# A decoder block on one core: the order of loads, diagonal operands and stores in its opening

## The chip, the core and the metric

The kernel runs on one core of a Trainium2 chip. The core has five engines that run their own queues of instructions side by side: TensorE (PE, with its weight loads as PEld) multiplies matrices, VectorE (DVE) and ScalarE (ACT) work element by element and read the PSUM banks that PE writes, GpSimd (POOL) works element by element on SBUF alone, and SyncE (SP) issues the transfers (DMAs). The metric is the device time of one execution in microseconds (us); smaller is better. All data is float32.

## What is computed

The reference takes x of shape (4, 2048, 512) and a context of shape (4, 77, 512) and applies one decoder layer of three parts, each on a layer norm and each added to x:

```python
x = x + recurrence(layernorm(x))      # step t: z = V (A*z + Vinv_dt x_t), output 2*Re(z); T=4 steps
x = x + cross_attention(layernorm(x)) # 16 heads of 32, 77 keys, softmax, Wq Wk Wv Wo (512x512)
h = layernorm(x) @ W_exp + b_exp      # 512 -> 2048
h = gelu(butterfly(h, up_weights) + up_bias)
x = x + butterfly(h, down_weights) @ W_con + b_con + down_bias
```

A butterfly is eleven stages of 2x2 mixtures over 2048 features. No non-linear step lies between W_exp and the first butterfly, nor between the second and W_con, so each pair is one 512x2048 or 2048x512 matrix, but this matrix has to be computed from its factors before it can be used.

## The kernel before

The 2048 rows of each of the four steps are worked on in 16 turns of 128 rows. `front` (L504) does the recurrence and the attention of a turn and makes the normalised input of the feed-forward part; `feed_forward` (L634) does the two large products. In turn u, `feed_forward(u)` is on PE while `front(u+1)` is advanced in small steps between its products (`step`, L643). All large products use Strassen's form with seven products in place of eight on half-sized blocks; the sums and differences of weight blocks that it needs are made once and kept in DRAM: `up7` (L769, one tensor for each of eight block columns, seven blocks each), `dn7` (seven tensors) and `wq7`.

Before the first turn can run there is an **opening** (L775 to L835). It makes the recurrence's taps (`_recurrence_taps`, L68), keys and values (`_keys_values`, L136), the two combined matrices (`_prepare`, L224) and the front of turn 0. All four are Python generators; each `next` on one of them emits its instructions up to its next `yield`. The lists of `run(...)` calls and the loop at L819 thus write the order out by hand. In this part PE, SP and POOL run in exactly that order (L775); DVE and ACT are ordered by the compiler's scheduler. After the opening PE is ordered by hand only for the first four block columns of turn 0 (L706).

`_prepare` goes through these steps:

- L285 to L293: W_exp is multiplied by the low seven butterfly stages; L299 to L305: transposes.
- L308 to L319: four groups g. For each, four PSUM banks are filled with products against `bd`, 16 diagonal matrices made at L298 by `diagonals` (L248), and evicted into `wup`, which then holds the first combined matrix. The turn counter in `evict` (L241) gives 2 of 5 evictions to DVE, 3 of 5 to ACT. SP loads a quarter of W_con after each group (L318).
- L321: `diagonals` once more, all 16 at once, into `bdd` for the second matrix. Their place is a tile of the tag `xt1` (L782).
- L330 to L344: the seven blocks of the first matrix. The first block of each column goes straight from `wup` to DRAM (L331, 8 transfers of 128 KB). For each of eight columns p, POOL (L335, L336) and DVE (L337, L338) make four sums in a ring of three places in `spare`, and SP stores them (L339, 512 KB). Two more blocks go straight out in 16 transfers (L343). `spare` is the room of the output weights `wo`, which are loaded later (L823).
- L346 to L353: 16 steps (n = 0 to 15 in the loop at L819) with `bdd`; L363 to L384: 16 steps (n = 16 to 31) of transposes L360 and products L369, with one group of four stores of sums every fourth step (`t1`, `t3`, `t2`, `n4` at L378 to L381, stores at L383). L385 closes it.

Beside it runs turn 0's front: its query product (`seven`, L488, evicted at L536 and L539), the scores (L557 to L567, row maxima and subtraction on DVE, exponent on ACT, scaling on POOL), the transposed probabilities `pt` (L575, tag `pt`, one buffer, shared with the query weights `wq`), the output product (evicted at L607) and a last norm (`norm_stats` L415, rows L446, transposes L455).

Then the preparation's pool is closed and others are opened in its room (L836 to L840): the activations, three weight buffers, and `ffn` with the tile `tb` of right-hand sums (`combine`, L622, L628 to L631). `up_head` (L665) takes a weight buffer and loads one block column of `up7` into it (L667), then emits the products 1, 6 and 5 of that column; the right side of product 1 is the normalised input itself, those of 6 and 5 are in `tb`. `up_mid` emits 2 and 7. The x of turn 1 is loaded at n = 18 (L829) into the place that `bdd` had.

```python
for n, _ in enumerate(prep):
    if n not in (3, 6, 9, 12, 23, 24, 25, 26):
        next(first, None)
    ...
    if n == 18:
        xts[1] = load_x(1)
```

Of the kernel before, what the change touches and what calls it, by code (L numbers as in the profile page):

```python
# [17 lines left out]
P = 128  # L18
# [49 lines left out]
def _recurrence_taps(nc, pool, psum, ssm_vec, ssm_vt, ssm_vinv, gt):  # L68


    vec = pool.tile([NS, 3], F32, name="vec")
    vt = pool.tile([NS, 3, NS], F32, name="vt")
    pz = pool.tile([NS, 2, 2 * NS], F32, tag="pz", bufs=2, name="pz")
    nc.sync.dma_start(out=vec, in_=ssm_vec)
    nc.sync.dma_start(out=vt[:, 0:2, :], in_=ssm_vt)
    nc.sync.dma_start(out=pz, in_=ssm_vinv)
    yield

    e = pool.tile([NS, 2], F32, name="e")
    _exp(nc, pool, e, vec[:, 0:2], 2)  # L80
    dt = e[:, 0:1]
    th = pool.tile([NS, 2], F32, name="th")
    nc.vector.tensor_tensor(th[:, 0:1], e[:, 1:2], dt, ALU.mult)
    nc.vector.tensor_scalar(th[:, 0:1], th[:, 0:1], -1.0, None, ALU.mult)
    nc.vector.tensor_tensor(th[:, 1:2], vec[:, 2:3], dt, ALU.mult)
    mag = pool.tile([NS, 1], F32, name="mag")
    _exp(nc, pool, mag, th[:, 0:1], 1)

    k = pool.tile([NS, 1], F32, name="k")
    r = pool.tile([NS, 2], F32, name="r")  # L90
    nc.vector.tensor_scalar(k, th[:, 1:2], 0.5 / math.pi, MAGIC, ALU.mult, ALU.add)
    nc.vector.tensor_scalar(k, k, -MAGIC, None, ALU.add)
    prev = th[:, 1:2]
    for c in _split(2.0 * math.pi, 8, 5):
        nc.vector.scalar_tensor_tensor(r[:, 0:1], k, -c, prev, ALU.mult, ALU.add)
        prev = r[:, 0:1]
    nc.vector.tensor_scalar(r[:, 0:1], r[:, 0:1], -3.1415925, 3.1415925, ALU.max, ALU.min)
    nc.vector.tensor_scalar(r[:, 1:2], r[:, 0:1], 0.5, None, ALU.mult)
    sn = pool.tile([NS, 2], F32, name="sn")
    nc.scalar.activation(sn, r, AF.Sin)  # L100
    az = pool.tile([NS, 2], F32, name="az")
    nc.vector.tensor_tensor(az[:, 0:1], sn[:, 1:2], sn[:, 1:2], ALU.mult)
    nc.vector.tensor_scalar(az[:, 0:1], az[:, 0:1], -2.0, 1.0, ALU.mult, ALU.add)
    nc.vector.tensor_tensor(az[:, 0:1], az[:, 0:1], mag, ALU.mult)
    nc.vector.tensor_tensor(az[:, 1:2], sn[:, 0:1], mag, ALU.mult)

    nc.vector.tensor_scalar(vt[:, 2, :], vt[:, 1, :], -1.0, None, ALU.mult)
    nc.vector.tensor_scalar(pz, pz, dt, None, ALU.mult)
    nc.gpsimd.memset(gt, 0.0)
    for j in range(T):  # L110
        ps = psum.tile([P, 512], F32, tag="c", name="ps_g")
        nc.tensor.matmul(ps[:, 0:NS], lhsT=pz[:, 0, :], rhs=vt[:, 0, :], start=True, stop=False)
        nc.tensor.matmul(ps[:, 0:NS], lhsT=pz[:, 1, :], rhs=vt[:, 2, :], start=False, stop=True)
        for h in range(2):
            if j + h < T:
                q = slice(h * NS, (h + 1) * NS)
                nc.vector.tensor_scalar(gt[q, j + h, :], ps[q, 0:NS], 2.0, None, ALU.mult)
        if j == T - 1:
            break
        rr = psum.tile([P, 512], F32, tag="f", name="ps_rr")[0:NS, 0 : 2 * NS]  # L120
        ri = psum.tile([P, 512], F32, tag="f", name="ps_ri")[0:NS, 0 : 2 * NS]
        nc.tensor.matmul(rr, lhsT=vt[:, 0, :], rhs=pz[:, 0, :], start=True, stop=False)
        nc.tensor.matmul(rr, lhsT=vt[:, 2, :], rhs=pz[:, 1, :], start=False, stop=True)
        nc.tensor.matmul(ri, lhsT=vt[:, 0, :], rhs=pz[:, 1, :], start=True, stop=False)
        nc.tensor.matmul(ri, lhsT=vt[:, 1, :], rhs=pz[:, 0, :], start=False, stop=True)
        nxt = pool.tile([NS, 2, 2 * NS], F32, tag="pz", bufs=2, name="pz_next")
        ti = pool.tile([NS, 2, 2 * NS], F32, tag="ti", name="ti")
        nc.vector.tensor_scalar(ti[:, 0, :], ri, az[:, 1:2], None, ALU.mult)
        nc.vector.scalar_tensor_tensor(nxt[:, 0, :], rr, az[:, 0:1], ti[:, 0, :], ALU.mult, ALU.subtract)
        nc.vector.tensor_scalar(ti[:, 1, :], rr, az[:, 1:2], None, ALU.mult)  # L130
        nc.vector.scalar_tensor_tensor(nxt[:, 1, :], ri, az[:, 0:1], ti[:, 1, :], ALU.mult, ALU.add)
        pz = nxt
        yield
# [90 lines left out]
def _prepare(nc, keep, pool, room, late, banks, dram, ident, wexp_t, up_low, up_high, up_bias, dn_low, dn_high, wcon,  # L224
# [11 lines left out]
    t = wdn  # L236
    mask = pool.tile([P, sub], F32, name="mask")
    nc.vector.tensor_reduce(mask, ident.rearrange("p (b i) -> p i b", i=sub), AX.X, ALU.add)
    turn = [0]

    def evict(out, ps):  # L241
        turn[0] += 1
        if turn[0] % 5 in (0, 2):
            nc.vector.tensor_copy(out, ps)
        else:
            nc.scalar.copy(out, ps)

    def diagonals(hp, place):  # L248
        for m in range(NB):
            keep(nc.vector.tensor_tensor(place[:, m, :].rearrange("p (b i) -> p b i", b=NB),  # L250
                                         hp[:, m, :].unsqueeze(2).to_broadcast([P, NB, sub]),
                                         mask.unsqueeze(1).to_broadcast([P, NB, sub]), ALU.mult))
        return [place[:, m, :] for m in range(NB)]
# [51 lines left out]
            yield  # L305
    el = _low_products(nc, keep, low, True, False)
    pb = banks()
    for g in range(4):  # L308
        for c in range(NC):
            ps = banks()  # L310
            for j in range(4):
                nc.tensor.matmul(ps.rearrange("p (k m) -> p m k", m=4)[:, j], lhsT=t[:, 4 * g + j, c * P : (c + 1) * P],
                                 rhs=bd[4 * g + j], start=j == 0, stop=True, skip_group_check=True)
            evict(wup[:, c, :].rearrange("p (k m) -> p k m", m=NB)[:, :, 4 * g : 4 * g + 4], ps.rearrange("p (k m) -> p k m", m=4))
        for j in range(4):
            m = 4 * g + j
            nc.tensor.matmul(pb[:, m : m + 1], lhsT=bd[m], rhs=b2[:, m : m + 1], start=True, stop=True)
        nc.sync.dma_start(out=t[:, 4 * g : 4 * g + 4, :], in_=wcon.rearrange("(p m) d -> p m d", m=NB)[:, 4 * g : 4 * g + 4, :])  # L318
        yield  # L319
    nc.vector.tensor_copy(b2, pb[:, 0:NB])  # L320
    bdd = diagonals(hp_dn, late())  # L321
    h, k = HID // 2, NC // 2

    def quarters(p):
        q = slice(p * P, (p + 1) * P)
        a11, a12 = wup[:, 0:k, q], wup[:, k:NC, q]
        q = slice(h + p * P, h + (p + 1) * P)
        return a11, a12, wup[:, 0:k, q], wup[:, k:NC, q]

    for p in range(NB // 2):  # L330
        nc.sync.dma_start(out=up7[p][:, 0], in_=quarters(p)[0])  # L331
    for p in range(NB // 2):
        a11, a12, a21, a22 = quarters(p)
        s = spare[:, p % 3 * 1024 : p % 3 * 1024 + 1024].rearrange("p (i k q) -> p i k q", i=4, k=k)
# [3 lines left out]
        nc.vector.tensor_tensor(s[:, 3], a12, s[:, 1], ALU.subtract)  # L338
        nc.sync.dma_start(out=up7[p][:, 3:7], in_=s)  # L339
        if p == NB // 2 - 1:  # L340
            for n in range(NB // 2):
                for i in (1, 2):
                    nc.sync.dma_start(out=up7[n][:, i], in_=quarters(n)[2 * i - 1])  # L343
        yield  # L344
    nc.sync.dma_start(out=brow[1, :].rearrange("(p m) -> p m", m=NB), in_=b2)
    for c in range(NC):  # L346
# [10 lines left out]
    def turned(b):  # L357
# [2 lines left out]
            nc.tensor.transpose(ps[:, c * P : (c + 1) * P], wup[:, c, b * P : (b + 1) * P], ident)  # L360
        evict(t[:, b, :], ps)

    for n in range(2):  # L363
        turned(order[n])
    for n, b in enumerate(order):
# [7 lines left out]
        if n % 4 == 3:  # L373
# [4 lines left out]
            nc.vector.tensor_tensor(t1, b12, b11, ALU.subtract)  # L378
            nc.gpsimd.tensor_tensor(t3, b22, b12, ALU.subtract)
            nc.vector.tensor_tensor(t2, b22, t1, ALU.subtract)  # L380
            nc.vector.tensor_tensor(n4, b21, t2, ALU.subtract)  # L381
            for i, w in ((0, b11), (1, b21), (2, b22), (4, t1), (6, t3), (5, t2), (3, n4)):
                nc.sync.dma_start(out=dn7[i][:, f, :], in_=w)  # L383
        yield  # L384
# [5 lines left out]
def kernel(ctx: ExitStack, tc: tile.TileContext, x, ctx_t, ssm_vec, ssm_vt, ssm_vinv, wq_t, wk_t, wv_t,  # L390
# [243 lines left out]
    def feed_forward(u, xt, rhs, other):  # L634
# [28 lines left out]
            nc.scalar.activation(out, x, AF.Gelu, bias=hbias[:, b : b + 1])  # L663

        def up_head(p):  # L665
            w = weights([P, 7, 2, P], "w_up")
            nc.sync.dma_start(out=w, in_=up7[p])  # L667
            a, b, c = (bank(g).rearrange("p (x t q) -> p x t q", x=2, q=P)[:, 0] for g in "abc")
            live[p] = (w, a, b, c)
            up(p, 1, a, True)  # L670
# [95 lines left out]
        turn[0] = (turn[0] + 1) % 3  # L766
        return psum.tile([P, 512], F32, tag="abc"[turn[0]], name="ps_p")

    up7 = [dram.tile([P, 7, 2, P], F32, name=f"up7_{p}") for p in range(NB // 2)]  # L769
    wq7 = dram.tile([P, 7, NC // 2, D // 2], F32, name="wq7")  # L770
    dn7 = [dram.tile([P, NB // 2, D // 2], F32, name=f"dn7_{i}") for i in range(7)]
    xts = {}
    ready = []
    E = mybir.EngineType
    with ExitStack() as stack, tc.manual_schedule(engines={E.PE, E.SP, E.Pool}):  # L775
        pool = stack.enter_context(tc.tile_pool(name="prep", bufs=1))
# [12 lines left out]
        def run(*gens):  # L789
            for g in gens:  # L790
                next(g, None)
# [5 lines left out]

        with tc.tile_pool(name="taps", bufs=1) as tp:
            taps = _recurrence_taps(nc, tp, psum, ssm_vec, ssm_vt, ssm_vinv, gt)
            run(taps, keys, prep, keys)  # L800
            xts[0] = load_x(0)
            next(prep)
            quarter_loads(wq, wq_t, (0, 1, 3, 6))
# [13 lines left out]
            run(prep, first)  # L817
        run(first, first)
        for n, _ in enumerate(prep):  # L819
            if n not in (3, 6, 9, 12, 23, 24, 25, 26):  # L820
                next(first, None)
            if n == 3:
                quarter_loads(wo, wo_t, (0, 1, 2, 6))  # L823
# [1 line left out]
                nc.gpsimd.tensor_tensor(wo[:, 6], wo[:, 2], wo[:, 6], ALU.subtract)  # L825
                nc.gpsimd.tensor_tensor(wo[:, 5], wo[:, 2], wo[:, 4], ALU.subtract)
                nc.gpsimd.tensor_tensor(wo[:, 3], wo[:, 1], wo[:, 5], ALU.subtract)
            if n == 18:
                xts[1] = load_x(1)  # L829
        for _ in first:  # L830
            pass
        db = work.tile([P, D], F32, tag="xn", name="db")
# [89 lines left out]
```

## Time and profile before

| | us |
|---|---|
| median of 3 runs (2638.39 to 2641.36) | 2640.1 |
| the profiled execution | 2640.16 |
| its span in the trace | 2638.4 |
| PE busy | 2566.2 (97%) |
| DVE busy | 1449.0 (55%) |
| POOL busy | 950.1 (36%) |
| ACT busy | 809.9 (31%) |
| DMA: 333.6 MB, share of the 16 engines on SP's queue | 36.0% |

The times inside the opening, from the timelines:

| event | us from the start |
|---|---|
| first product of keys (L150) starts | 9.07 |
| the matmuls L312 of the first matrix start | 83.30 |
| the diagonals for the second matrix (L250), DVE | 101.35 |
| the scores of turn 0 (L557) start | 119.2 |
| the products L350 of the second matrix start | 130.6 |
| the load of the x of turn 1 is issued | 172.07 |
| last product of the output projection ends | 190.0 |
| last preparation product on PE ends | 212.1 |
| first feed-forward product starts | 224.55 |

How to read it: busy time of PE is modelled and includes pipelining, so what is worth looking for is not its share but the places where PE stands still, and what ended each wait. A line of a timeline gives start and length in us, engine, source line, operation, output<-inputs, shape and count; in brackets stands how long the engine had been idle before it, and the instruction whose end released it. Where an instruction waits for several events, only the one that came last by the profile is named, and it can be the wrong one. The granted clock of PE is given in tenths of full speed.

### The profile page before, as it was taken

Reading aid. Unit: us, or ns where it says so; the run is one execution under the profiler, and the core shown is the slowest. Engines: PE = TensorE matmul, PEld = TensorE weight load, DVE = VectorE, ACT = ScalarE, POOL = GpSimd, SP = SyncE. Lnnn points to the kernel's source line nnn. Section 1 sums busy time; section 2 is a strip of 40 time slices with the busy share of each in tenths; the row PEclk is TensorE's granted clock in tenths of the full one; section 3 lists DMA queues with packets and bytes.
Section 4 is the critical chain, followed back from the end, with each engine's and each line's share of the span. In section 5 each row is a group of like instructions: output and inputs, shape, how many; then the busy total and the mean of one; then the engine's idle time right before and its main releaser. Section 6 shows DMA issues by size and latency. Waiting matters only on the chain.

```text
span 2638.4 us, 37437 instructions
## 1 busy us (share of the span) xinstructions
PE 2566.2 (97%) x14536; PEld 2182.0 (83%) x14536; DVE 1449.0 (55%) x3355; ACT 809.9 (31%) x1470; POOL 950.1 (36%) x1025
## 2 busy tenths in 40 slices
PE   7887999999999999999999999999999999999999
PEld 5775888888888888888888888888888888888888
DVE  6666645545564554556455455645545564554531
ACT  2332414124241412424141342414234241423420
POOL 4332342515234251523425152342515234251523
PEclk9898999999999999999999999999999999999999
DMA  5536243242424324242432424233242423323243
GB/s 177 199 109 211 93 136 132 87 150 96 160 92 136 132 87 150 96 160 92 136 132 87 150 97 160 92 134 132 88 150 97 160 92 133 131 91 134 96 133 139
DMA packets 95394, 333.60 MB, mean 126 GB/s; under 512 B 15601, under 2 KB 49521, under 8 KB 78065
## 3 DMA queue, kind: packets, MB, share of 16 engines
q1 hardware_dynamic: 95218, 331.21, 36.0%
q8 instruction: 116, 1.90, 0.3%
q14 instruction: 60, 0.49, 0.1%
HBM read 297.61 MB, written 33.57 MB: 126 GB/s over the span
## 4 chain that ended last, share of the span: by engine, by line
PE 83%; DVE 6%; ACT 5%; issue 1%; DMA 0%; ACTq 0%; DVEq 0%; SPq 0%
PE ps_a L726 13%; PE ps_b L658 10%; PE ps_b L726 8%; PE ps_w L499 7%; PE ps_a L658 7%; PE ps_c L658 7%; PE ps_q L499 7%; PE ps_c L726 6%; PE ps_sc L557 5%; PE ps_pt L579 4%; PE ps_s L514 3%; PE ps_o L589 2%; PE ps_t L455 2%; ACT L563 1%; ACT L663 1%; DVE st L420 1%
## 5 line engine op out<-in xcount | busy, mean ns | idle before, releaser
L658 PE MATMUL ps_b<-tb,w_up 128*128 128x256 f32 x1536 | 397.7, 380 | 0.0
L726 PE MATMUL ps_a<-w_dn,a 128*128 128x256 f32 x1536 | 373.0, 380 | 0.0
L701 POOL TENSOR_TENSOR s<-a,a 128x256 f32<-128x256 f32 x128 | 93.0, 727 | 675.9 <-ACT a L663 453.5
L658 PEld LDWEIGHTS ps_b<-tb,w_up 128*128 128x128 f32 x1536 | 287.7, 190 | 39.4
L663 ACT ACTIVATE a<-a,hbias 128x256 f32<-128x256 f32 x384 | 193.6, 508 | 406.5 <-DVE a L696 277.2
L726 PEld LDWEIGHTS ps_a<-w_dn,a 128*128 128x128 f32 x1536 | 282.4, 190 | 41.6 <-issue 3.0
L658 PE MATMUL ps_a<-xnt,w_up 128*128 128x256 f32 x1024 | 264.2, 381 | 12.0 <-DMA w_up<-up 12.0
L726 PE MATMUL ps_c<-w_dn,s 128*128 128x256 f32 x1024 | 248.6, 379 | 0.0
L456 ACT COPY xnt<-ps_t 128x512 f32<-128x512 f32 x128 | 73.7, 587 | 523.1 <-PE ps_t L455 523.1
L567 POOL TENSOR_TENSOR pr<-pr,sm 128x1232 f32<-128x1232 f32 x64 | 144.0, 2250 | 248.8 <-DVE sm L566 243.9
L658 PEld LDWEIGHTS ps_a<-xnt,w_up 128*128 128x128 f32 x1024 | 192.0, 191 | 37.9 <-issue 12.2
L726 PEld LDWEIGHTS ps_c<-w_dn,s 128*128 128x128 f32 x1024 | 188.7, 190 | 27.8
L607 DVE TENSOR_TENSOR xt<-ps_w,xt 128x512 f32<-128x512 f32 x96 | 66.1, 689 | 213.6 <-PE ps_w L499 147.0
L557 PE MATMUL ps_sc<-kbd,qt 128*128 128x308 f32 x512 | 174.4, 439 | 5.9 <-DVE pr L562 5.7
L714 POOL TENSOR_TENSOR xt<-xt,ybias 128x256 f32<-128x256 f32 x128 | 99.4, 810 | 223.1 <-DVE xn L446 223.0
L563 ACT ACTIVATE pr<-pr 128x308 f32<-128x308 f32 x256 | 111.1, 457 | 136.2 <-DVE pr L562 135.7
L579 PE MATMUL ps_pt<-ident,pr 128*77 128x128 f32 x1024 | 143.8, 276 | 8.6 <-ACT a L663 4.7
L499 PE MATMUL ps_q<-xnt,wq 128*128 128x256 f32 x640 | 151.4, 380 | 0.0
L579 PEld LDWEIGHTS ps_pt<-ident,pr 128*77 128x77 f32 x1024 | 117.6, 147 | 40.5 <-ACT a L663 11.0
L499 PEld LDWEIGHTS ps_q<-xnt,wq 128*128 128x128 f32 x640 | 122.1, 191 | 16.7
L672 ACT COPY p<-ps_a 128x256 f32<-128x256 f32 x128 | 47.7, 373 | 277.7 <-PE ps_a L658 277.7
L658 PE MATMUL ps_c<-tb,w_up 128*128 128x256 f32 x512 | 132.5, 381 | 0.0
(199 smaller groups left out, 4586.5 us busy)
## 6 DMA issues: line engine op xcount, KB each, us to landing
w_up<-up SPq DMA_DIRECT2D x128, 896.0 KB, 4.6
w_dn<-dn SPq DMA_DIRECT2D x112, 1024.0 KB, 4.8
wq<-wq SPq DMA_DIRECT2D x16, 1792.0 KB, 8.5
xt<-in_x SPq DMA_DIRECT2D x16, 1024.0 KB, 5.3
out<-xt SPq DMA_DIRECT2D x64, 256.0 KB, 4.7
wdn<-in_wexp_t SPq DMA_DIRECT2D x4, 1024.0 KB, 10.3
wdn<-in_wcon SPq DMA_DIRECT2D x4, 1024.0 KB, 5.1
up<-wo SPq DMA_DIRECT2D x8, 512.0 KB, 2.6
```

The costliest lines, as they stand in the source:

```text
L456: nc.scalar.copy(xnt[:, :, t, :], ps)
L499: nc.tensor.matmul(tiles[key][:, r, :], lhsT=lhs(i, r, k), rhs=rhs(i, r, k), start=key == i and r == 0 and k == 0, stop=k == 1, skip_group ...
L514: nc.tensor.matmul(ps[:, 2 * i : T, f * NS : (f + 1) * NS], lhsT=xpt[:, i, c * (P // NS) + f, :], rhs=gt[:, 0 : T - 2 * i, :], start=i == ...
L557: nc.tensor.matmul(ps[:, 0 : 4 * NK], lhsT=qt[:, g, t, :], rhs=kbd[:, t, g, :], start=True, stop=True)
L563: nc.scalar.activation(pg, pg, AF.Exp, scale=1.0 / math.sqrt(DH))
L567: nc.gpsimd.tensor_tensor(pr, pr, sm.unsqueeze(2).to_broadcast([P, NH, NK]), ALU.mult)
L579: nc.tensor.transpose(pt_ps[0:NK, j, :], pr[:, 4 * g + j, :], ident)
L658: nc.tensor.matmul(ps, lhsT=w[:, c, :], rhs=rhs[i - 1][:, c], start=first and c == 0, stop=c == 1, skip_group_check=True)
L663: nc.scalar.activation(out, x, AF.Gelu, bias=hbias[:, b : b + 1])
L701: nc.gpsimd.tensor_tensor(s1, a21, a22, ALU.add)
L714: nc.gpsimd.tensor_tensor(r, r, ybias[:, d], ALU.add)
L726: nc.tensor.matmul(ps[:, t, :], lhsT=act[p][lhs[i]][:, t, :], rhs=w[:, p, :], start=first and p == 0 and t == 0, stop=p == h - 1, skip_gro ...
```

## The change

It touches the opening, and one place in `up_head`.

- The generator of the taps yields once more after the load of `vec`, and the first `run` calls it twice: the loads of the context and of Wk are issued between `vec` and the other two.
- `diagonals` can make some of the 16. Those for the second matrix are made in four lots of four, each at the head of one of the four groups of the loop at L308.
- `up7` becomes one DRAM tensor. A function `plain` stores one of the three unchanged blocks for all eight columns in two transfers (one for each half of the contraction): 6 transfers in place of 24.
- From the last 16 steps on, DVE gets 2 of 6 evictions in place of 2 of 5. The last of the four differences, `n4`, goes from DVE to POOL.
- In the loop over n the steps at which the front is not advanced change: 4, 8, 12 and 22 to 26 in place of 3, 6, 9, 12 and 23 to 26.
- At n = 17 the weights of the first block column are loaded into a tile of the tag `pt`; `up_head` takes them in place of a weight buffer and a load, once. The x of turn 1 is loaded after the loop.

```diff
     nc.sync.dma_start(out=vec, in_=ssm_vec)
+    yield
     nc.sync.dma_start(out=vt[:, 0:2, :], in_=ssm_vt)
...
-    turn = [0]
+    turn, share = [0], [5]
...
-        if turn[0] % 5 in (0, 2):
+        if turn[0] % share[0] in (0, 2):
...
-    def diagonals(hp, place):
-        for m in range(NB):
+    def diagonals(hp, place, some=slice(0, NB)):
+        for m in range(NB)[some]:
...
+    place = late()
     for g in range(4):
+        bdd = diagonals(hp_dn, place, slice(4 * g, 4 * g + 4))
         for c in range(NC):
...
-    bdd = diagonals(hp_dn, late())
...
-    for p in range(NB // 2):
-        nc.sync.dma_start(out=up7[p][:, 0], in_=quarters(p)[0])
+    def plain(i, c, x):
+        for n in range(k):
+            nc.sync.dma_start(out=up7[:, :, i, n, :].rearrange("b p q -> p b q"),
+                              in_=wup[:, c + n, x : x + h].rearrange("p (b q) -> p b q", q=P))
+
+    plain(0, 0, 0)
...
-            for n in range(NB // 2):
-                for i in (1, 2):
-                    nc.sync.dma_start(out=up7[n][:, i], in_=quarters(n)[2 * i - 1])
+            plain(1, k, 0)
+            plain(2, k, h)
...
+    share[0] = 6
     for n in range(2):
         turned(order[n])
...
-            nc.vector.tensor_tensor(n4, b21, t2, ALU.subtract)
+            nc.gpsimd.tensor_tensor(n4, b21, t2, ALU.subtract)
...
-            w = weights([P, 7, 2, P], "w_up")
-            nc.sync.dma_start(out=w, in_=up7[p])
+            if early:
+                w = early.pop()
+            else:
+                w = weights([P, 7, 2, P], "w_up")
+                nc.sync.dma_start(out=w, in_=up7[p])
...
-    up7 = [dram.tile([P, 7, 2, P], F32, name=f"up7_{p}") for p in range(NB // 2)]
+    up7 = dram.tile([NB // 2, P, 7, 2, P], F32, name="up7")
...
-            run(taps, keys, prep, keys)
+            run(taps, keys, taps, prep, keys)
...
-            if n not in (3, 6, 9, 12, 23, 24, 25, 26):
+            if n not in (4, 8, 12, 22, 23, 24, 25, 26):
...
-            if n == 18:
-                xts[1] = load_x(1)
+            if n == 17:
+                early.append(work.tile([P, 7, 2, P], F32, tag="pt", bufs=1, name="w_first"))
+                nc.sync.dma_start(out=early[0], in_=up7[0])
+        xts[1] = load_x(1)
```

More of the change, by code (lines that the diff above doesn't have):

```diff
@@ L773 @@
     ready = []
+    early = []
     E = mybir.EngineType
```

## The prediction

> **What bounds the kernel now.** I read the 40 slices first, then the table of stretches, then the timelines of PE (TensorE), DVE (VectorE), POOL (GpSimd) and SP (the DMA queue) over the first 260 us, and last the chain of waits around the stalls found there. From the page, the slices of PE and its granted clock:
>
> ```profile
> PE   7887999999999999999999999999999999999999
> PEclk9898999999999999999999999999999999999999
> ```
>
> Only the first four slices (66 us each) are below 9. The table (columns: stretch; length, busy us and counts of PE, weight loads, DVE, ACT, POOL; clock, DMA share, GB/s) says where:
>
> ```profile
> 100.00:120.00 20.00, 14.76 (x62) 12.07 (x61) 13.87 (x32) 2.46 (x3) 9.88 (x13) 0.83 0.56 187
> 120.00:140.00 20.00, 13.80 (x82) 8.63 (x82) 16.57 (x36) 5.25 (x11) 7.60 (x6) 0.83 0.52 184
> 200.00:220.00 20.00, 8.09 (x33) 4.64 (x31) 14.46 (x42) 4.59 (x8) 3.78 (x3) 0.84 0.77 228
> 260.00:400.00 140.00, 139.64 (x801) 119.18 (x801) 75.14 (x167) 44.24 (x79) 52.60 (x53) 1.00 0.31 108
> ```
>
> From 260 us on PE is full, and the change edits none of that work. What can move is the opening: 26 us of PE idle in three 20-us stretches. The timelines name three stalls of PE. **Stall 1**, at 104.8:
>
> ```profile
> 109.88 3.75 PE L499 MATMUL ps_q<-tq,wq 128*128 128x256 f32 x8 [5.09 <-DVE qt L536]
> ...
> 101.35 7.44 DVE L250 TENSOR_TENSOR bd<-hp_dn,mask 128x128 f32<-128x128 f32 x16
> ```
>
> PE waits for the eviction L536, which stands on DVE behind all 16 diagonal products. **Stall 2**, at 201.4, waits for normalised rows L446 at the end of a DVE queue without a gap; **stall 3**, at 212.6, for the first FFN weights:
>
> ```profile
> 205.92 0.66 PE L455 MATMUL ps_t<-ident,xn 128*128 128x128 f32 x4 [4.50 <-DVE xn L446]
> 224.55 2.04 PE L658 MATMUL ps_a<-xnt,w_up 128*128 128x256 f32 x4 [11.97 <-DMA w_up<-up]
> ```
>
> The chain of waits shows what precedes stall 3's end, and DVE's timeline what else stood there:
>
> ```profile
> 215.64 3.66 DMA dn<-wup
> ...
> 219.45 4.97 DMA w_up<-up
> ...
> 219.72 0.69 DVE L628 TENSOR_TENSOR tb<-xnt 128x512 f32<-128x512 f32 x1 [3.82 <-DMA ybias<-in_b_con]
> 220.44 1.63 DVE L630 TENSOR_TENSOR tb<-xnt,tb 128x512 f32<-128x512 f32 x1
> ```
>
> The reader should see that not only the weights but also tb, the right sides of the second and third product, start just after the last dn7 store has landed (219.3). New pools take the room of the closed preparation pool; I read both as waiting for its release, and the name ybias as a bystander (it lands near 221).
>
> **Part 1, order of the first loads.** vec, ct, wk, then vt and pz. Two issues of 0.6 us each go behind wk: ps_k may start 1.2 us earlier than 9.07. At 43.7 PE waits 2.0 us for rows that need POOL's L210, fed by high, whose place in the queue is unchanged. The 1.2 us become a longer wait there: worth 0 (0 to 1.2).
>
> **Part 2, diagonals in four lots.** The 16 products (7.44 us, 0.46 each) move into the loop L308. There DVE idles 1.99 us before most of its six evictions and is busy 0.69 in each, 4.1 us of 17.8; 7.4 more fit. hp_dn lands about 84.7 (issue 82.70 + 2.0), 1.5 us after the first PE group starts. A lot holds an eviction for 4 x 0.46 = 1.9 us; PE fills a bank each 0.9 us and has six. At nothing, then; were DVE late, PE would pay at most one lot, 1.9.
> After it L536 follows product 6 at once. Stall 1 goes: 5.09. The eight matmuls after it took 3.54 to their successor against 1.73 for eight warm ones, the next 24 5.75 against 5.2: 2.4 more. PE reaches the scores (119.2) **7.4 us** earlier.
> Next late is DVE: over 119.2 to 130.6 it carries 16 score operations and the row sums, and eight L337/L338 products of 0.41 pushed there by the diagonals (3.3 us). With the first pair at 102 instead of 108.7, about five of those eight run before the scores: 2.1 us. I take **1.5**, ends -2 and 3, since the spare ring of three must drain through a DMA queue already full of wcon.
>
> **Part 3, up7 as one tensor, 24 stores as 6.** SP spends 5.5 + 9.0 us issuing the 24; six at about 0.5 to 1.0 us take 3 to 6. Nobody waits for SP there except the first L339 issue, which in fact waited for DVE. Bytes and 512-byte pieces are unchanged. Nothing by itself. If overlaps in one tensor were judged coarsely, the L339 stores would wait for plain(0); that is rival B.
>
> **Part 4, later evictions 1 in 3 instead of 2 in 5 on DVE, n4 to POOL, xt1 later, statistics one step earlier.** Between the last w product (190.0) and the rows (205.3) DVE has no gap, so every operation removed counts. Removed: three xt1 statistics with aggregates 2.1; two n4 of 0.6; about one eviction 0.6. Before it, the n4 at 186.8 took 1.63 beside POOL and held the add at 188.37 by 1.2. Together 5.1. The skip list runs the last products and statistics one step of 1.3 us earlier against the transposes. 6.4 against 4.50 (+0.59 at 198.4): stall 2 goes. Its cold aftermath goes too: from 205.92 to 211.99 PE took 6.07 for 4.33 of warm work. Full gain 6.8; I take **6.0**, low end 2.5 (DVE order still unlucky).
> Two evictions of 0.59 per three fall to ACT, which idles half of that stretch.
> Against n4 on POOL stands the GPSIMD Engine Reference of the Trainium skill (4.1 Engine selection): two-input elementwise work belongs on VectorE, GpSimd being about twice as slow. The rows, in the last group:
>
> ```profile
> 212.85 1.77 POOL L379 TENSOR_TENSOR wup<-wdn 128x512 f32<-128x512 f32 x1 [8.73 <-DVE y L433]
> ...
> 213.53 1.63 DVE L381 TENSOR_TENSOR wup<-wdn,wup 128x512 f32<-128x512 f32 x1
> ```
>
> Alone, POOL's 1.27 (L379 at 196.2) is indeed twice DVE's 0.68. By the rule the last n4 is worse by 0.6 plus its place behind t3: ready at 214.4 + 1.27 = 215.7 against 215.16. By the rows DVE itself loses 0.95 when both run, so 0.5 is all that the tail pays; taken below.
>
> **Part 5, weights early.** w_first needs the last read of pt (L589 ends 166.5) and up7, stored by about 150; issued by SP before the first dn7 stores, it lands some 40 us before use. Let E = 212.1 be the end of PE's last preparation product. Before: product 1 at E+12.4, product 6 at E+14.25, product 7 done at E+19.96. After: xnt is ready at E+1.1, product 1 runs E+1.1 to 2.9. Then PE waits for t2: dn7 landed at E+7.7 (0.5 for n4), L628 and L630 done at E+10.4. Products 6, 5, 2, 7 follow. xt1 now lands after the stores, at about E+9.5 (1 MB; 9.1 us when contended); its statistics and rows take about 7 us of DVE after tb, E+17.5, and PE wants them at E+18.
> TensorE: Matmul & The Clock Gate (Part 1, the HAM clock gate) speaks against counting the whole gap: after an idle window of 3.4 us PE runs at half rate, and wakes after about 3.4 us of sustained work. 7.5 us of idle remain, so the slow spell stays. By the row it lasts longer: the four groups after stall 3 take 2.04, 1.71, 1.71, 1.23 against 0.86, clock 0.50 until about 230.6, 6 us. By the rule the four products end at E+15.6, a gain of 4.4; by the row 1.71 x 3 + 1.3 gives E+16.8, a gain of 3.2. I take **3.6**, the row with tb's DVE work somewhat quicker once stall 2's backlog is gone. Ends 0 and 6.
>
> **Sum.** 7.4 + 1.5 + 6.0 + 3.6 = 18.5. The profiled execution took 2640.16 (span 2638.4 and 1.8 around it), the median of the runs is 2640.1: 2621.6.
>
> **Rivals.**
> A. The end of stall 3 is taken over by xt1 (0.12). DVE is not ordered by hand: its queue may hold xt1's statistics ahead of tb. tb would then be ready near E+17.5 and product 6 start 3 us later than before. For it: rows of xt1 stand before tb on DVE now (215.17). Against: tb is written first. Gain 18.5 - 3.6 - 3.3 = 11.6: 2628.5.
> B. The middle gives some back (0.13). Stores into one up7 wait for each other, or the ring does; L337/L338 pile up among the scores again and PE loses 3.5 of the 7.4 and the 1.5. Gain 13.5: 2626.6.
> C. tb does not wait for the release (0.08): the 3.82 before it are then of another cause that moves along. Stall 3 goes wholly: 11.97 and the cold 3.25 instead of 3.6. Gain 30: 2610.
> D. Slower (0.07). One buffer fewer is drawn in the first turn, so all later loads of the 16 turns use the three weight buffers one place shifted, and everything outside PE, SP and POOL is ordered anew. At 1.2 us a turn the 15 later turns eat 18 us; at 1.8 it is 27 us, net +8.5: 2648.5. For it: PE has no slack there (139.64 of 140). Against: 15 loads a turn are a multiple of three, and the buffers are alike.
>
> **How the numbers follow.** The forecast has 0.60. Its own bounds: 5.1 - 2 + 2.5 + 0 = 5.6 and 7.4 + 3 + 6.8 + 6 + 1.2 = 24.4, both unlikely together; 2615 to 2632 holds nearly all of it, and A and B. Left out are C and D. No change is anything within 0.2%, 5.3 us. Faster: all of C, nearly all of A, B and the forecast, 0.90; D 0.07; same 0.03.
>
> **What would show it.** Right: no PE wait for L536 near 105 and scores starting about 112; no wait for L446 longer than 1 us; one PE wait of 6 to 8 us after the first up product, ended by tb, with the clock at half after it; xt1 landing before 230. Wrong: a wait for w_up of the second or first pair, PE idle for xp rows after the first up products, DVE idle at a diagonal while PE waits, or turns after 260 us that are not of the old length.

## The result, and the profile after

| | before | after |
|---|---|---|
| median of 22 runs each, us | 2640.38 | 2635.31 |
| lowest to highest | 2638.39 to 2641.98 | 2630.78 to 2638.05 |
| span of the profiled execution | 2638.4 | 2633.6 |
| PE busy | 2566.2 | 2565.4 |

The ratio is 0.9981 (95% interval 0.9974 to 0.9987): 5 us less, where 18.5 were forecast. The page's slices after:

```profile
PE   8887999999999999999999999999999999999999
PEclk9998999999999999999999999999999999999999
```

The fourth slice (198 to 263 us) is as poor as before. The table of stretches (columns as before):

```profile
80.00:100.00 20.00, 17.08 (x139) 16.81 (x138) 14.15 (x24) 6.35 (x11) 8.97 (x6) 0.91 0.54 204
100.00:120.00 20.00, 17.49 (x95) 14.19 (x94) 13.63 (x23) 3.50 (x5) 11.17 (x14) 1.00 0.78 266
...
200.00:220.00 20.00, 8.76 (x36) 6.10 (x35) 10.03 (x15) 5.47 (x9) 11.10 (x9) 0.74 1.00 338
...
260.00:400.00 140.00, 139.64 (x798) 119.29 (x798) 74.79 (x164) 42.76 (x77) 54.09 (x55) 1.00 0.34 116
```

Stage 100 to 120 gained 2.7 us of PE work, 80 to 100 has a hole that was not there (PE was at 20.00), 200 to 220 is hardly better (8.76 for 8.09), and from 260 us on nothing changed. PE's timeline names the new holes:

```profile
90.37 4.42 PE L315 MATMUL ps_p<-wo,wdn 128*128 128x128 f32 x24 [2.92 <-DVE wup L245]
...
108.76 1.96 PE L505 MATMUL ps_q<-tq,wq 128*128 128x256 f32 x8 [0.70 <-DVE qt L542]
...
197.23 1.10 PE L375 MATMUL ps_p<-wdn,low_dn 128*128 128x512 f32 x2 [1.57 <-DVE wdn L245]
...
216.50 2.05 PE L664 MATMUL ps_b<-tb,w_first 128*128 128x256 f32 x4 [11.24 <-DMA ybias<-in_b_con]
...
227.14 1.11 PE L490 MATMUL ps_t<-ident,xp 128*128 128x128 f32 x4 [3.60 <-DVE xp L479]
```

Stall 1 shrank from 5.09 to 0.70. Stall 2, 4.50 for rows, is gone; what is left near its place is 1.57 for an eviction. New are 2.92 in the first matrix's loop (L315 is L312 of before) and 3.60 for turn 1's rows; stall 3 is 11.24 instead of 11.97, one product later.

So that all runs can be compared, I cut PE's timeline at six marks: start of the first matrix's matmuls, start of the query's product 6, scores, first matmul with `bdd`, end of the last preparation matmul (E, here the transposes' modelled end), and the first recurrence matmul of turn 1. The stages between them, in us, each from the one profiled execution of the kernel (the medians are of all its runs):

| kernel | loop over g | query | scores | `bdd` to E | E to turn 1 | median |
|---|---|---|---|---|---|---|
| before | 17.8 | 18.1 | 11.4 | 82.0 | 28.0 | 2640.4 |
| after | 22.4 | 11.6 | 11.9 | 76.6 | 31.1 | 2635.3 |
| e1 lots late | 17.8 | 11.6 | 12.4 | 76.5 | 30.9 | 2629.2 |
| e2 x early | 23.4 | 11.6 | 12.5 | 78.0 | 25.1 | 2632.7 |
| e3 second pool | 23.6 | 11.6 | 12.5 | 76.5 | 30.7 | 2635.6 |
| e4 = e2 and e3 | 22.1 | 11.6 | 11.8 | 78.1 | 22.1 | 2626.8 |
| e5 one lot | 17.8 | 18.3 | 11.0 | 79.9 | 29.5 | 2637.9 |
| e7 = e1, e4, two columns | 17.8 | 11.6 | 11.9 | 78.2 | 20.7 | 2620.9 |
| e8 weights alone | 17.8 | 18.3 | 11.3 | 82.5 | 24.1 | 2636.9 |
| e9 few stores | 23.7 | 11.6 | 12.5 | 76.5 | 31.3 | 2635.8 |
| e10 = e7, n4 on DVE | 17.8 | 11.6 | 12.3 | 80.8 | 19.7 | 2623.2 |
| e11 no low products | 17.8 | 11.6 | 11.8 | 76.7 | 30.9 | 2630.6 |
| e12 n4 on DVE | 23.9 | 11.6 | 12.5 | 76.2 | 31.1 | 2636.0 |

The change's account: 1.4 gained before the first mark, -4.7, +6.5, -0.4, +5.4, -3.1: 5.1. The two negative stages, the loop over g and the tail, took 7.8 us back. The loop's loss is not the same in every profile: the six kernels with the lots at all four groups beside the chain (after, e2, e3, e4, e9, e12) take 22.1 to 23.9 us in it, 4.3 to 6.1 more than before.

### The profile page after: what moved, and what is told of

Same layout as the page of the kernel before. It is cut to its first block, busy times and chain, and to the rows that moved or that the text cites. A ratio compares the mean times of both kernels' runs of the same rounds, so it can differ in the third digit from the quotient of the medians.

```text
span 2633.6 us, 37429 instructions
## 1 busy us (share of the span) xinstructions
PE 2565.4 (97%) x14536; PEld 2181.7 (83%) x14536; DVE 1454.5 (55%) x3349; ACT 810.9 (31%) x1472; POOL 955.2 (36%) x1029
## 4 chain that ended last, share of the span: by engine, by line
PE 86%; DVE 7%; ACT 4%; issue 1%; DMA 1%; POOL 0%; SPq 0%; ACTq 0%; DVEq 0%; POOLq 0%
PE ps_a L735 13%; PE ps_b L664 10%; PE ps_b L735 9%; PE ps_w L505 7%; PE ps_q L505 7%; PE ps_c L664 7%; PE ps_a L664 7%; PE ps_c L735 6%; PE ps_sc L563 5%; PE ps_pt L585 4%; PE ps_s L520 3%; PE ps_o L595 2%; PE ps_t L461 2%; ACT L569 1%; DVE st L426 1%
## 5 line engine op out<-in xcount | busy, mean ns | idle before, releaser
L723 POOL TENSOR_TENSOR xt<-xt,ybias 128x256 f32<-128x256 f32 x128 | 99.3, 811 | 223.1 <-DVE xn L452 223.0
```

The lines of the kernel that those rows point to most:

```text
L723: nc.gpsimd.tensor_tensor(r, r, ybias[:, d], ALU.add)
```

## The experiments

### Where the loop over g lost 4.7 us: e1, e11, e5

DVE's timeline and the same stretch by form (columns: line, engine, operation, shapes, count; busy us, mean ns; idle) of the changed kernel:

```profile
83.04 6.67 DVE L251 TENSOR_TENSOR bd<-hp_dn,mask 128x128 f32<-128x128 f32 x4 [0.23 <-DMA hp_dn<-hscr]
...
90.23 0.88 DVE L251 TENSOR_TENSOR bd<-hp_dn,mask 128x128 f32<-128x128 f32 x4
```

```profile
L186 POOL TENSOR_TENSOR low_dn<-low_dn 128x2048 f32<-128x2048 f32 x1 | 4.2, 4194 | 0.1
```

The first lot takes 6.67 us, the second 0.88. POOL's chain L186 runs from 79.74 to 89.36. The four diagonals of the first lot last 2193, 278, 4151 and 278 ns; the two long ones stand beside the chain's last two products, of 2132 and 4194 ns, and end with them. e1 puts the lots where the chain has ended.

```diff
-        bdd = diagonals(hp_dn, place, slice(4 * g, 4 * g + 4))
+        if g >= 2:
+            bdd = diagonals(hp_dn, place, slice(8 * g - 16, 8 * g - 8))
```

> The changed kernel, but the diagonals are made in two lots of eight, at groups 2 and 3 of the loop over g, so that none meets POOL's chain of low products L186 (79.7 to 89.4 in the changed kernel). Theory (a DVE product with two SBUF inputs stands still beside that chain): all 16 take about 0.22 us each, 3.5 in sum, the first too; PE's 2.9 us wait inside L315 and its cold aftermath vanish, product 6 of the query starts near 99.8 instead of 104.4, about 4.5 us less than the changed kernel, if nothing later absorbs it. Rival (the lots are too much work for DVE in this loop, or the first lot is slow of itself): the first diagonal is again long, or PE waits as long at group 2 or 3; less than 1.5 us gained.

2629.2 us (ratio to before 0.9959, 0.9946 to 0.9971), 6 less than the changed kernel, where 4.5 were expected. DVE's timeline of e1:

```profile
91.46 1.70 DVE L251 TENSOR_TENSOR bd<-hp_dn,mask 128x128 f32<-128x128 f32 x8
```

Eight diagonals in 1.70: 0.21 each, and the loop is back at 17.8 us. e11 leaves the lots where the change put them and leaves out the chain, that is, the low products of the second matrix:

```diff
-    el = _low_products(nc, keep, low, True, False)
+    el = low[:, nlow - NB * P : nlow].rearrange("p (b x) -> p b x", b=NB)
```

> The changed kernel without POOL's chain of low products for the second matrix (the second matrix is then wrong); the lots of four stay at groups 0 to 3. Theory (the first lot stands still beside that chain): the first four diagonals take 0.9 us as the other lots do instead of 6.7, L315 takes 17.8 us instead of 22.4. Rival (the first lot is slow by its place, through hp_dn or the bank it blocks): it stays at 4 us or more and PE waits again.

```profile
83.45 0.90 DVE L251 TENSOR_TENSOR bd<-hp_dn,mask 128x128 f32<-128x128 f32 x4 [0.65 <-DMA hp_dn<-hscr]
```

The same lot at the same place, still waiting for the same transfer, now takes 0.90, and the loop 17.8 (2630.6 us in its one run). Place, bank and `hp_dn` are ruled out; the chain is the cause. e5 undoes the lots and keeps the rest:

```diff
-        bdd = diagonals(hp_dn, place, slice(4 * g, 4 * g + 4))
...
     nc.vector.tensor_copy(b2, pb[:, 0:NB])
+    bdd = diagonals(hp_dn, place)
```

> The changed kernel with the diagonals in one lot of 16 behind the loop, as before the change; all else changed. Theory (the lots cost 4.7 us inside L315 beside POOL's chain and bring 6.5 us between product 6 and the scores): L315 takes 17.8 us again and product 6 to scores 18.1 instead of 11.6, so that it is 1.8 us slower than the changed kernel. Rival (the lots are a loss, the early weights bring all of the gain): 2 us or more faster than the changed kernel.

2637.9 us (0.999, 0.9984 to 0.9997), 2.6 slower than the changed kernel, with 17.8 and 18.3 as expected. The lots thus bring about half of the change's 5 us: in the two stages that they touch a gain of 6.5 pays for a loss of 4.7. The table also shows 3.3 more between `bdd` and E, which the expectation did not have. In that profile the output product of the first step runs at half rate (32 matmuls in 1.93 us, 1.08 in the changed kernel); the rest I did not trace.

### Where the tail lost: e2, e3, e4, e8, e9

SP's timeline of the changed kernel, and DVE's first line of `tb`:

```profile
205.73 3.01 SPq L389 DMA_DIRECT2D dn<-wup  x4
208.83 0.68 SPq L418 DMA_DIRECT2D xt<-in_x  x1
```

```profile
213.73 0.69 DVE L634 TENSOR_TENSOR tb<-xnt 128x512 f32<-128x512 f32 x1 [7.17 <-DMA dn<-wup]
```

The last store is issued at 208.06 and `tb` starts 5.7 us later; before it was 215.64 and 4.1. Behind the store now comes the x of turn 1, 1 MB. Its statistics start only at 216.0, and PE waits for the rows at 223.5. e2 loads this x where it was:

```diff
             if n == 17:
                 early.append(...)
                 nc.sync.dma_start(out=early[0], in_=up7[0])
+            if n == 18:
+                xts[1] = load_x(1)
-        xts[1] = load_x(1)
```

> The changed kernel, but turn 1's x is loaded at n = 18 as before the change, behind the early weights. Theory (the load behind the stores makes turn 1's rows late): PE's 3.6 us wait for xp near 223.5 and the slow matmuls behind it (1.6) vanish; three statistics go back to DVE in the stretch before the last transposes, where PE's 1.6 us wait grows to 2 or 3.5; in all 2 to 4 us less than the changed kernel. Rival (the rows are late because DVE holds the eviction u before the statistics and POOL slows the small operations): the wait for xp stays above 2 us, gain under 1 us.

2632.7 us (0.997, 0.9958 to 0.9981), 2.6 less. E to turn 1 fell by 6.1, `bdd` to E grew by 1.4 (the statistics that went back to DVE), and this run's loop over g happened to be 1.0 longer, the first lot meeting POOL's chain a little differently. PE has no wait for xp. The store's wait shrank too; SP's and DVE's timelines of e2:

```profile
209.35 2.54 SPq L389 DMA_DIRECT2D dn<-wup  x4
```

```profile
215.51 1.80 DVE L634 TENSOR_TENSOR tb<-xnt 128x512 f32<-128x512 f32 x1 [3.57 <-DMA ybias<-in_b_con]
```

From the last issue (211.5) to `tb` it is 4.0 us. In every kernel with one pool and the x behind the stores it is 5.4 to 5.7 (the changed kernel, e1, e5, e9, e11, e12), in every one with one pool and the x ahead 4.0 to 4.1 (before, e2, e8). The changed kernel and e2 differ in the place of this load alone.

e9 asks whether the stores of the earlier groups, which follow each other faster now, are a second cause. They are left out, and the same rows of dn7 filled once before the transposes:

```diff
+    for i in range(7):
+        nc.sync.dma_start(out=dn7[i][:, 0:6, :], in_=spare[:, 0:1536].rearrange("p (x y) -> p x y", x=6))
...
-            for i, w in ((0, b11), ..., (3, n4)):
+            for i, w in ((0, b11), ..., (3, n4))[(0 if n > 11 else 7):]:
```

> The changed kernel without the dn7 stores of the first three of four groups; in their place the same rows are filled once from another buffer before the transposes begin, when the DMA queues are nearly idle, so that the second matrix is wrong. Theory (four groups of 1.8 MB follow each other faster than the queues drain, and this backlog delays the last store, tb and turn 1's x): product 6 starts 10.4 us after the last preparation product instead of 12.1, x lands about 2 us earlier, and the wait for xp shrinks to about 2 us. Rival (the last group alone, or the fixed time of a store, sets it): product 6 stays at 11.5 us or later.

My theory fell (one run, 2635.8 us). Between 164.4 and 203.57 SP issued no transfer, and still product 6 starts 11.6 us after E (12.1 in the changed kernel), the last store takes 5.5 to release `tb`, and the wait for xp is 3.55. The last group and the x behind it are enough.

e3 asks what `tb` waits for. Everything of the preparation but `wup` and `wdn` goes to a second pool, into whose room `tb` then falls:

```diff
         wdn = pool.tile([P, NB, D], F32, name="wdn")
+        pool = stack.enter_context(tc.tile_pool(name="prep2", bufs=1))
```

> The changed kernel, but everything of the preparation except wup and wdn lies in a second pool, so that tb falls into the room of that pool and does not wait for the stores that read wup and wdn. Theory (tb waits for the whole closed pool, 11.2 us of PE): tb starts about 1 us after the last preparation product of PE and product 6 follows product 1 within 3 us; the next wait is then for the second column's weights, behind the stores on the DMA queue, and for xp, whose x still lands near 216, so that the whole gains only 0 to 2 us. Rival (tb waits for something else, such as ybias): product 6 starts 12 us after the last preparation product as in the changed kernel.

```profile
208.40 1.65 DVE L634 TENSOR_TENSOR tb<-xnt 128x512 f32<-128x512 f32 x1
...
211.82 2.04 PE L664 MATMUL ps_b<-tb,w_first 128*128 128x256 f32 x4 [4.81 <-issue]
...
221.35 1.53 PE L664 MATMUL ps_a<-xnt,w_up 128*128 128x256 f32 x4 [4.21 <-DMA w_up<-up]
```

`tb` starts at 208.40, before the last store has even been issued (209.53), and product 6 starts 5.7 us after E instead of 12.1: the release of the whole closed pool was what held `tb`. It is not the 3 us that were expected: DVE is busy with the last differences until then, and its first operation of `tb` takes 1.65 beside POOL's last difference and part of `tb`, instead of 0.69. And the whole gains nothing (2635.6; 0.9981, 0.9972 to 0.999): PE then waits 4.21 for the second column's weights and 3.10 for xp, and the slow clock comes twice. e4 adds the early x:

> Both edits of the two kernels before: the second pool, and turn 1's x loaded at n = 18. Theory: tb is early, xp rows are early, and the only wait left in the first up products is that for the second column's weights, landing about 6 us after product 7; 5 to 8 us less than the changed kernel. Rival: the stores on the DMA queue set the end whatever waits for what, and it gains no more than the early x alone.

2626.8 us (0.9948, 0.9936 to 0.9961), 8.6 less than the changed kernel. Alone, the pool was worth 0 and the early x 2.6: the pool's gain appears only when nothing else is late behind it. A wait of 1.16 for the second column's weights is left.

e8 is the early weights alone, on the kernel before:

```diff
-            w = weights([P, 7, 2, P], "w_up")
-            nc.sync.dma_start(out=w, in_=up7[p])
+            if early:
+                w = early.pop()
+            else:
+                w = weights([P, 7, 2, P], "w_up")
+                nc.sync.dma_start(out=w, in_=up7[p])
...
+            if n == 17:
+                early.append(work.tile([P, 7, 2, P], F32, tag="pt", bufs=1, name="w_first"))
+                nc.sync.dma_start(out=early[0], in_=up7[0])
             if n == 18:
                 xts[1] = load_x(1)
```

> The kernel before, with the early weights of the first column alone (loaded at n = 17 into the room of the probabilities); turn 1's x stays at n = 18, the diagonals in one lot, the stores as before. Theory (in the changed kernel the tail is worse because PE's earlier end meets the same stores, and because x comes behind them): here tb starts 7.6 us after the last preparation product and product 6 about 10.3 after it, against 13.8 before; no wait for xp; 3 to 4.5 us less than the kernel before. Rival (the release itself costs what the weights did): product 6 again 12 us or more after the last preparation product, gain under 1.5 us.

2636.9 us (0.9985, 0.9978 to 0.9992), 3.5 less than before; product 6 at E + 9.6 (13.8 before). The early weights do what was forecast for them, when the x does not stand behind the stores.

### What n4 on POOL is worth: e12, e10

Both put n4 back on DVE, e12 in the changed kernel, e10 in the best one (below).

```diff
-            nc.gpsimd.tensor_tensor(n4, b21, t2, ALU.subtract)
+            nc.vector.tensor_tensor(n4, b21, t2, ALU.subtract)
```

> The changed kernel with n4 on DVE as before the change. Theory (n4 on POOL takes 0.6 us per group off DVE in the stretch where it is full, and costs 0.6 at the end): the stretch from the last w product to the last preparation product grows by 0.5 to 1.5, the time from there to product 6 falls by 0.5; within 1.5 us of the changed kernel. Rival (n4 behind t3 on POOL is what makes the last store late): 2 us or more faster.

> The kernel with the late lots, the second pool, the early x and two early weight columns, but with the difference n4 on DVE as before the change. Theory (with tb free of the stores, POOL's n4 no longer delays PE except where POOL and DVE share the work at the end): DVE carries 0.6 us more per group before the last transposes, that stretch grows from 19.7 to 20.5 us, tb itself is made a little earlier because POOL's t3 and n4 no longer run beside it; within 1 us of the kernel with n4 on POOL. Rival (n4 on POOL was a gain of its own): 2 us or more slower.

e12 is at 2636.0 (0.9983, 0.9977 to 0.999), 0.7 from the changed kernel, too little to tell from nothing. The stretch from the last product of the output projection to E did not grow by the 0.5 to 1.5 that were expected (18.0 against 18.2). In e10 it grew by 2.7 instead of 0.8 (22.4 against 19.7 in e7), with a wait of 3.69 for the rows, and the time to product 6 shrank by 1.1: 2623.2 against 2620.9. That is the size that the rival of this expectation named, not the theory's; but the five runs of each overlap (2620.8 to 2625.2, 2620.5 to 2622.2), so the stages show it more firmly than the medians. The difference between the two pairs is that turn 1's statistics stand on DVE before E in e7 and e10 and behind it in the changed kernel and e12. In these profiles n4 on POOL shortens the stretch only where DVE carries those statistics too.

The four kernels form a square, in the stage from `bdd` to E: 80.8 with x early and n4 on DVE (e10, as before the change), 78.2 with n4 on POOL alone (e7), 76.2 with x late alone (e12), 76.6 with both (the changed kernel). They differ in other edits too (e7 and e10 have the late lots and the second pool); e2, which differs from the changed kernel in x alone, has 78.0. So the two moves overlap, and what they leave to the later evictions and the earlier step is, by the kernel before, about 82.0 - 80.8 = 1.2 us.

### A version that beats both: e7

e1, e2 and e3 together, and the second column's weights in the other half of the same room:

```diff
+                two = work.tile([P, 2, 7, 2, P], F32, tag="pt", bufs=1, name="w_first")
+                for i in range(2):
+                    nc.sync.dma_start(out=two[:, i], in_=up7[i])
+                early.extend((two[:, 1], two[:, 0]))
```

> The changed kernel with the lots of eight at groups 2 and 3, the second pool, turn 1's x loaded at n = 18, and the weights of two columns loaded early into the room of the probabilities. Theory (the costs found are separate and add): 4.4 us from L315, 9 us from the tail and about 1 us for the second column's wait: 2621 to 2623. Rival (one covers the other: stores or a later stage take back what each frees): not under 2626.

2620.9 us, ratio to before 0.9924 (0.991 to 0.9937), just under the 2621 to 2623 that were expected if the costs add. PE's longest wait in its tail:

```profile
207.76 2.04 PE L665 MATMUL ps_b<-tb,w_first 128*128 128x256 f32 x4 [4.75 <-issue]
```

What is left there is the time in which DVE and POOL make the last differences and `tb` beside each other.

## Why the prediction was wrong, step by step

- **The reading** of three stalls, and of the turns as untouched, was right: 260 to 400 us has the same 139.64 us of PE. So was the reading of `tb` as bound by the closed pool (e3).
- **Part 1** was costed at 0; the first mark came 1.4 earlier (81.92 for 83.30), and between 80.4 and 82.6 in all kernels with the new order. The first product of the keys starts at 7.31 for 9.07, and the wait that was to absorb this grew only from 2.03 to 2.46: POOL's L210, which the rows behind it were said to need and which was taken as unchanged, ended at 41.5 for 42.9. This gain was not foreseen.
- **Part 2, "at nothing", is the first term that failed.** The room on DVE was there, as counted. But 0.46 us a diagonal was taken from a place where POOL ran operations of 0.73 us, and I put it beside POOL operations of up to 4.19 without looking at POOL's row for the same stretch, though the trace of before has the end of that chain there:

```profile
83.38 7.54 POOL L185 TENSOR_TENSOR low_dn<-low_dn 128x512 f32<-128x512 f32 x3
```

  Part 4 counted this very effect, 0.95 lost by DVE beside a POOL operation of 1.77; part 2 did not. My limit of one lot, 1.9, was wrong for the same reason. Measured: a lot of 6.67, for PE a wait of 2.92 and slow matmuls behind it (clock 0.91 in the row of 80 to 100, 1.00 before), 4.7 in sum.
- **Stall 1** gave 6.5 of 7.4, **scores** -0.4 of 1.5: the bound from below was -2. The forecast counted eight of the sums L337 and L338 among the scores and moved five of them ahead; the trace of before has six there (119.2 to 130.6), and the changed kernel has six again (116.0 to 127.8), as the fourth column's sums still waited 3.01 for a place in the ring.
- **Part 3** cost nothing that shows, and coarse judging of overlaps (rival B's main cause) did not occur: in the changed kernel the first of the L339 stores is issued at 108.09, just as its last sum is made (108.02).
- **Part 4** gave 5.4 of 6.0 from the first `bdd` matmul to E. The number is nearly right, its parts are not, and that is luck. The sum added what overlaps: by the square above x is worth 1.4 (78.0 in e2) and n4 nothing where the other has been moved, but 4.6 and 2.6 where it has not; 2.1 and 2.4 were counted. The later evictions and the earlier step, counted as 1.9, bring about 1.2 by the same square; neither was tried alone.
- **Part 5, 3.6, is the second term that failed**: -3.1. The early weights themselves brought 3.5 (e8). What was mis-sized is the line "turn 1's x lands at E+9.5, its rows at E+17.5, PE wants them at E+18". It left no margin. Counted, as the forecast does, from the end of the last preparation product (203.95), `tb` starts at E+9.8, the rows are there at E+23, and PE wants them at E+19.6. The x delayed the store before it by 1.6 and so `tb`; and from the end of DVE's part of `tb` (216.09) to the rows it took 11.0 us where about 7 were counted, as DVE held an eviction of product 6 between the statistics and then had small operations beside POOL's additions L723:

```profile
218.65 0.42 DVE L684 TENSOR_TENSOR u<-ps_b,p 128x256 f32<-128x256 f32 x1 [1.96 <-PE ps_b L664]
```

  PE waited 3.60, and its clock fell a second time. Moving the x cost 6.1 in the tail and saved 1.4 before it.
- **The clock.** After 11.2 us of idle the slow groups took 2.05 and 1.74, and the granted clock (the third figure from the right) was back at 1.00 from about 219.8 on, 3.3 us after product 6 had started:

```profile
216.00:218.00 2.00, 1.50 (x4) 1.26 (x5) 0.69 (x2) 0.00 (x0) 1.83 (x2) 0.50 0.99 400
218.00:220.00 2.00, 2.00 (x7) 1.61 (x6) 1.35 (x4) 0.00 (x0) 1.92 (x3) 0.55 1.03 388
220.00:222.00 2.00, 2.00 (x11) 1.77 (x10) 1.93 (x7) 0.47 (x1) 2.00 (x4) 1.00 1.07 417
```

  The forecast took the longer slow spell of the trace of before, 6 us, over the 3.4 us of the page TensorE: Matmul & The Clock Gate in the Trainium skill (Part 1). Both lengths occur. The rule was nearer here; with it the term would have been 4.4, still a gain.
- **Rivals and signs.** No rival happened as written. A named the right transfer, but thought that x would pass `tb` on DVE; it came behind it and made the rows late instead. Of B the loss of the 1.5 came true. Nothing speaks for D. Two of the signs that the forecast gave for being wrong came: PE idle for xp rows, and DVE at a diagonal while PE waits.

Together: 18.5 - 4.7 - 6.7 (tail) - 0.6 - 0.9 - 1.9 + 1.4 = 5.1. e7 repairs both failed terms and adds the second pool and a second column of early weights; with all four the kernel is 19.5 faster than before. The two repairs without the additions were not run together.

## What to carry to other kernels

Before an operation is moved into the idle time of DVE, look at what POOL does at that moment: idle time beside a long two-input POOL operation is not free to a DVE operation that reads two SBUF operands. A transfer that is moved behind others because it is "not needed yet" has two costs, its own consumer's and that of the stores ahead of it, so leave a margin at both. And where several transfers and releases end close together, removing one is worth nothing until the next is removed too (0, 2.6, and 8.6 for both).

## What was unexpected of the hardware

A DVE operation can stand still for a whole POOL operation rather than run slower beside it: a diagonal of 0.21 us (e1) lasted 4151 ns beside POOL's product of 4194 ns, while PSUM evictions between 80 and 83 us kept their 0.69 beside the same chain. SBUF — State Buffer in the Trainium skill (SBUF: two separate sides) says this: the pair of ports that both use is held exclusively for an instruction. The runs agree for products with two SBUF operands; that I did not weigh it against part 2 is the failed step. Smaller operations are held too: DVE's operations on 128x4 elements, 0.16 us elsewhere, took 0.64 to 0.77 each from 221.6 to 224.3, beside POOL's eight additions L723, and 0.15 again when these had ended:

```profile
218.74 5.51 POOL L723 TENSOR_TENSOR xt<-xt,ybias 128x256 f32<-128x256 f32 x8
...
223.63 0.64 DVE L437 TENSOR_TENSOR w<-y,v 128x4 f32<-128x4 f32 x1
...
225.18 0.15 DVE L437 TENSOR_TENSOR w<-y,v 128x4 f32<-128x4 f32 x1
```

And `tb` starts 1.3 to 1.7 us later after the issue of the last 256 KB store when a 1 MB load stands behind that store on the queue than when it does not (5.4 to 5.7 us against 4.0 to 4.1). Why the load delays it the runs do not show.
